# A two-layer block on one core: where powers, tables, quantised tiles and statistics stand among the projections

## The chip, the core and the metric

The kernel runs on one core of a Trainium2 chip. The metric is the device time of one execution in microseconds. The core has five engines that run side by side: TensorE (PE) multiplies matrices into PSUM, VectorE (DVE), ScalarE (ACT) and GpSimd (POOL) work on tiles in SBUF, and SyncE (SP) issues most transfers. Each engine runs its own list of instructions strictly in order.

## The reference, cut to what matters

The input `x` has 2 sequences of 4096 tokens with 512 channels. Layer 0 adds to `x` a gated state-space branch and a linear layer on quantised data; layer 1 adds a linear attention and a gated feed-forward part.

```python
xn = _layernorm(x, axis=-1)
# branch 1
x1 = xn @ w1_w.T + w1_b
x_conv = _silu(_depthwise_conv(x1, conv_w))        # three taps along the tokens
x_ssm = _ssm(x_conv, A, B_ssm, C_ssm, D_ssm)       # h = h*sigmoid(A) + x*B;  y = C.h + D*x
v = _silu(xn @ v1_w.T + v1_b)
branch1 = x_ssm * v @ w2_w.T + w2_b
# branch 2: rows of xn and of weight, rounded to 6-bit numbers by blocks of 32 with one scale each
branch2 = dequantised(xn) @ dequantised(weight).T + bias
x = x + branch1 + branch2
# layer 1 follows: layernorm, linear attention, gated feed-forward
```

## The kernel before, in words

All data is 32-bit. The tokens are cut into `NK` = 16 blocks of `T` = 512. The first stage, the projections, goes over the blocks `n`; after it come the recurrence (four groups of channels), and then for each sequence the mixing of both branches and layer 1. The change concerns the first stage alone, some 480 us of the 2400.

In block `n`, `projected` (L338) multiplies the normalised and transposed block `xnT` by `w1` and then by `v1`. Each product is four groups of 128 output channels; a group is gathered in one of four PSUM accumulators (`acc`) and copied out by ACT: `x1` (L351) for the first product, `v` with its Silu (L366) for the second. `tapped` (L394) makes the convolution of the block before: one ACT copy (L397), two DVE multiply-adds (L399), a Silu on ACT (L406), a DVE transpose (L408) and a store to `cd`. `halo` (L335) copies one column between neighbouring blocks on POOL.

Around the products, the other work of the stage:

- `fetched` (L290) loads the four token tiles of a block, three blocks ahead in the text. `measured` takes the mean and variance of two blocks (`layernorm_stats`, L123 and L124, and the chain of `rstd`, with a root on ACT, L110). `spread_out` (L132, L134) stores these numbers to DRAM and reads them back in another order into `mvi`.
- `laid` (L317) loads the same block a second time, in an order in which 32x32 transposes give the whole transpose. `turned` (L320) scales it on ACT by `mvi` (L128, sixteen pieces a block) and transposes it on DVE (L324, four a block) into the next `xnT`. Block 0 alone is transposed by TensorE.
- `chunk_powers` is a generator in three steps: powers of sigmoid(A) into `pw`; products of these in `cp` with sums and a store; then 64 small reads from DRAM into `a32` and `qc` (L252, L255). `chunk_tables` (L262, L266) transposes the results into tables `ta` and `tb` for the recurrence, one call for each of four groups of channels.
- `quantised_weight` quantises one of four tiles of branch 2's weight, and `quantised` one tile of 128 tokens; here the twelve tiles of blocks 0, 1 and 2. Both use `mx_scaled` (DVE L176 to L179, POOL L180) and `mx_rounded` (DVE L188 to L193, POOL L194).

Tiles of a pool with the same tag share a fixed number of places, handed out in the order of the text; a tile waits until the place it is to take is free. Tag `w` has four places of 8 KB a partition. Two hold `w1` and `v1` during the stage. The other two are taken in turn by `xi` of blocks 1 and 2 and then by `pw` and `cp`; `xi` of later blocks lies in two places of its own (tag `xi`). Tag `yv` has eight places, four of them taken by `xd0`, four left for tiles that are being quantised.

The order in each engine's list is not that of the text. A planner runs ahead of time over the whole program with its own estimates of durations: for each engine it takes, among the instructions that it believes ready, the one that stands earliest in the text. Later work thus fills free time, often some blocks ahead. Where a call stands in the loop therefore sets its rank and not its time, and the finished lists are kept even where the chip's times differ from the estimates.

The loop before:

```python
x1 = projected(work, n, xnT, x1)
if n % 2 == 0 and n + 2 < NK:
    measured(n + 2, xts.pop(n + 2) + xts.pop(n + 3))
    ...
if n + 1 < NK:
    xnT = turned(work, n + 1, xi)
if n in (2, 3, 8):
    next(powers)
elif 4 <= n < 4 + CC:
    chunk_tables(*made, n - 4)
    quantised_weight(work, n - 4)
if 6 <= n < 6 + 2 * TJ:
    ...                                   # one tile of blocks 0 and 1 each
if n in (NK - 3, NK - 2):
    ...                                   # two tiles of block 2 each
```

Of the kernel before, what the change touches and what calls it, by code (L numbers as in the profile page):

```python
# [10 lines left out]
F32 = mybir.dt.float32  # L11
# [6 lines left out]
P = 128  # L18
D = 512
CC = D // P  # L20
T = 512
TJ = T // P
# [21 lines left out]
def block_kernel(ctx: ExitStack, tc: tile.TileContext, a: dict, out: bass.AP):  # L44
# [5 lines left out]
    NK = B * NB  # L50
# [11 lines left out]
    single = ctx.enter_context(tc.tile_pool(name="single", bufs=1))  # L62
# [18 lines left out]
    def acc():  # L81
        return bank("acc", 4)
# [75 lines left out]
    def by_tile(wide):  # L158
        return wide[:, 0 : TJ * D].rearrange("p (j c t) -> p j c t", j=TJ, t=P)
# [100 lines left out]
    def chunk_tables(pw, kr, cc):  # L260

        nc.vector.transpose(  # L262
            window(ta[:, cc, 0, L - 1 : L], [[-1, L], [L, L]]),
            window(kr[:, cc, 0:1], [[1, L], [1, L]]),
        )
        nc.vector.transpose(  # L266
            tb[:, cc].rearrange("p c s -> p s c"),
            window(pw[:, cc * NS, L - 1 : L], [[L, NS], [-1, L]]),
        )
# [40 lines left out]

    def laid(work, n):

        if n < 3:
            xi = wp.tile([P, TJ, D], F32, tag="w", name="xi")
        else:
            xi = work.tile([P, TJ, D], F32, tag="xi", name="xi")
        nc.sync.dma_start(out=xi, in_=a["xi"][n * TJ : (n + 1) * TJ].rearrange("j p d -> p j d"))  # L317
        return xi

    def turned(work, n, xi):  # L320
        xnT = work.tile([P, CC, T], F32, tag="xnT", name="xnT")
        for j in range(TJ):
            laid_normalised(xi[:, j, :], mvi[:, :, n, j, :])
            nc.vector.transpose(  # L324
                xnT[:, :, j * P : (j + 1) * P], xi[:, j, :].rearrange("p (c t) -> p c t", t=P)
            )
        return xnT
# [11 lines left out]
    def projected(work, n, xnT, before):  # L339

        x1 = work.tile([P, CC, T + 2], F32, tag="x1", name="x1")
        tapping = []

        def finish():
            while tapping:
                tapping.pop(0)()

        for o in range(CC):
            pm = acc()
            product(pm, lambda k: w1[:, k, o * P : (o + 1) * P], lambda k: xnT[:, k, :])  # L350
            nc.scalar.activation(x1[:, o, 1 : T + 1], pm, AF.Identity, bias=w1_b[:, o, :])  # L351
            halo(n, o, x1, before)

            finish()
            if n:
                tapping.append(tapped(work, n - 1, before, o))
            if n == NK - 1 and o:

                tapping.append(tapped(work, n, x1, o - 1))
        if n == NK - 1:  # L360
            tapping.append(tapped(work, n, x1, CC - 1))
        for o in range(CC):
            pm = acc()
            product(pm, lambda k: v1[:, k, o * P : (o + 1) * P], lambda k: xnT[:, k, :])
            v = work.tile([P, T], F32, tag="v", name="v", bufs=3)
            nc.scalar.activation(v, pm, AF.Silu, bias=v1_b[:, o, :])  # L366
            nc.scalar.dma_start(out=vd[n, o], in_=v)
            finish()
        return x1

    def quantised_weight(work, o):
        y = yv.tile([P, D], F32, tag="yv", name="w_y")
        nc.sync.dma_start(out=y, in_=a["ffn_w"][o])
        s = mx_scaled(y)
        mx_rounded(y, s, work.tile([P, D], F32, tag="xe", name="w_c"))
        nc.vector.transpose(wd[:, :, o * P : (o + 1) * P], y)
# [625 lines left out]
    with tc.tile_pool(name="tab", bufs=1) as tab:  # L1002
        ta = tab.tile([P, CC, L, L], F32, name="ta")
        tb = tab.tile([P, CC, L, NS], F32, name="tb")
        qc = tab.tile([P, CC, L // 2, L], F32, name="qc")
        with pool("a", 2) as work, pool("pm", 1) as pm:
            xts = {0: fetched(work, 0)}
            w1 = load_weight("w1_w")
            ident = const.tile([P, P], F32, name="ident")
            make_identity(nc, ident)  # L1010
            w1_b = column("w1_b")
            v1 = load_weight("v1_w")
            v1_b, conv_w = column("v1_b"), column("conv_w", 3)
            xi = laid(work, 1)
            measured(0, xts[0])
            xnT = first_turned(work, xts.pop(0))
            xts[1] = fetched(work, 1)
            measured(1, xts.pop(1))
            spread_out(mvi[:, :, 1], sd[1], mv0[:, 1])
            xts[2] = fetched(work, 2)  # L1020
            spread_out(mvi[:, :, 0], sd[0], mv0[:, 0])
            d_ssm = column("D_ssm")
            abar, cb, b_ssm = (column(s, NS, pm) for s in ("A", "C_ssm", "B_ssm"))
            a32 = const.tile([P, CC, L // 2], F32, name="a32")
            ones = const.tile([P, 1], F32, name="ones")
            nc.gpsimd.memset(ones, 1.0)
            wd = const.tile([P, CC, D], F32, name="w_d")

            mask = const.tile([P, QC], F32, name="mask")
            nc.vector.tensor_reduce(  # L1030
                mask, ident.rearrange("p (q t) -> p q t", q=QC), AX.X, ALU.add
            )
            mask_c = const.tile([P, QC], F32, name="mask_c")
            nc.vector.tensor_reduce(
                mask_c, ident.rearrange("p (u q s) -> p q u s", u=2, q=QC), AX.XY, ALU.add
            )
            x1 = None
            made = []
            powers = chunk_powers(pm, made)
            xd0 = [yv.tile([P, CC, P], F32, tag="yv", name=f"xd{j}") for j in range(TJ)]  # L1040

            def quantise(m, j, dst):
                for _ in quantised(
                    m, j, dst, lambda: work.tile([P, D], F32, tag="xe", name="c")
                ):
                    pass

            for n in range(NK):
                if 0 < n < NK - 1:
                    xi = laid(work, n + 1)  # L1050
                if n + 3 < NK:
                    xts[n + 3] = fetched(work, n + 3)
                x1 = projected(work, n, xnT, x1)
                if n % 2 == 0 and n + 2 < NK:
                    measured(n + 2, xts.pop(n + 2) + xts.pop(n + 3))
                    for m in (n + 2, n + 3):
                        spread_out(mvi[:, :, m], sd[m], mv0[:, m])
                if n + 1 < NK:
                    xnT = turned(work, n + 1, xi)
                if n in (2, 3, 8):  # L1060
                    next(powers)
                elif 4 <= n < 4 + CC:
                    chunk_tables(*made, n - 4)
                    quantised_weight(work, n - 4)
                if 6 <= n < 6 + 2 * TJ:

                    m, j = divmod(n - 6, TJ)
                    if m == 1 and j == 0:
                        xd_b1 = by_tile(single.tile([P, CC * (T + 1)], F32, name="wide"))
                    quantise(m, j, lambda: xd_b1[:, j] if m else xd0[j])  # L1070
                if n in (NK - 3, NK - 2):

                    for j in range(2):
                        quantise(2, 2 * (n - NK + 3) + j, None)
                if n == NK - 2:
                    b_out = load_row("w2_b")
                    ffn_b = work.tile([P, D], F32, tag="xe", name="ffn_b")
                    nc.sync.dma_start(out=ffn_b, in_=a["ffn_b"].partition_broadcast(P))
                    nc.gpsimd.tensor_tensor(b_out, b_out, ffn_b, ALU.add)
                    bk, gamma, beta = (load_row(s) for s in ("bk", "gamma", "beta"))  # L1080
                    bq, mu_r, mu_k = column("bq"), column("mu_r"), column("mu_k")
                    om_r = const.tile([P, CC, 1], F32, name="om_r")
                    om_k = const.tile([P, CC, 1], F32, name="om_k")
                    nc.vector.tensor_scalar(om_r, mu_r, -1.0, 1.0, ALU.mult, ALU.add)
                    nc.vector.tensor_scalar(om_k, mu_k, -1.0, 1.0, ALU.mult, ALU.add)
        heads = [yv.tile([P, TL, L], F32, tag="yv", name=f"head{i}") for i in range(2)]
        with pool("s", 2) as work:
            recurrence(work, heads)
# [10 lines left out]
    for b in range(B):  # L1099
# [4 lines left out]
        made = (gt, ksum, load_weight("Wv"))  # L1104
        wq, wk1 = load_weight("Wq"), load_weight("W_k")
        c_wts = []
        if b + 1 < B:
            xd0 = [yv.tile([P, CC, P], F32, tag="yv", name=f"xd{j}") for j in range(TJ)]
# [90 lines left out]
```

## Time and profile before

| | |
|---|---|
| time, median of 3 runs | 2401.54 us (2398.27 to 2402.26) |
| profiled execution | 2401.88 us, span of the program 2400.1 us |
| busy share PE, DVE, ACT, POOL | 98%, 64%, 42%, 20% |
| projections on TensorE | 13.86 to 479.93 us |

Times inside the profile count from the start of the span. A row gives the start, the length, the engine, the line of the program, the operation, what it writes and reads, and how often it stands there in a row; in brackets is the time the engine was idle before it and who released it. TensorE takes each 32-bit product in two passes, so that the sixteen products of a half block show as `x32`.

### The profile page before, as it was taken

To read this page: it belongs to the slowest core of one execution; us is meant where nothing else is said; L and a number is where in the kernel's file an instruction comes from. 1 tells how busy PE (TensorE), PEld (TensorE's weight loads), DVE (VectorE), ACT (ScalarE), POOL (GpSimd) and SP (SyncE) were. 2 spreads that over 40 slices of the span, in tenths; PEclk is the share of its full clock that TensorE was granted. 3 is DMA by queue.
4 is the path that set the end of the run, shared out by engine and by line. 5 is a ranking of instruction groups with operands and counts; after the bars stand their busy time and mean duration, and the time that the engine had idled before them with its cause. 6 is when DMAs were issued, how large, how long until landed. Compare 5 with 4: busy or idle time off the path is not lost. (4 is left out here: it accounts for less than half of the span.)

```text
span 2400.1 us, 21969 instructions
## 1 busy us (share of the span) xinstructions
PE 2357.7 (98%) x6400; PEld 1105.2 (46%) x6400; DVE 1532.0 (64%) x3050; ACT 1018.5 (42%) x1933; POOL 477.8 (20%) x534
## 2 busy tenths in 40 slices
PE   7999999999999999999999999999999999999999
PEld 3334444466544444444444555444444444445554
DVE  6976864554486664257768778666652265557777
ACT  6766775334242333246763222133332236652222
POOL 0211220022143332110103112233332100001111
PEclk9999999999999999999999999999999999999999
DMA  7647432377843333202255435433432202264331
GB/s 262 197 130 229 137 141 96 115 223 251 317 132 113 110 117 94 67 28 104 92 210 194 149 134 189 165 108 115 119 110 75 62 31 88 90 217 141 126 133 57
DMA packets 253832, 328.12 MB, mean 137 GB/s; under 512 B 55952, under 2 KB 117392, under 8 KB 252688
## 3 DMA queue, kind: packets, MB, share of 16 engines
q1 hardware_dynamic: 224624, 259.59, 34.3%
q10 hardware_dynamic: 29088, 67.12, 7.2%
q8 instruction: 51, 0.84, 0.1%
q14 instruction: 69, 0.57, 0.1%
HBM read 205.38 MB, written 121.27 MB: 136 GB/s over the span
## 5 line engine op out<-in xcount | busy, mean ns | idle before, releaser
L154 PE MATMUL p_acc<-xnT,w_v_w 128*128 128x512 f32 x512 | 227.4, 600 | 9.1 <-ACT x L351 9.1
L154 PE MATMUL p_acc<-xnT,w_w_w 128*128 128x512 f32 x512 | 225.2, 597 | 9.4 <-DVE xnT L324 5.0
L698 PE MATMUL p_acc<-k,x 128*128 128x512 f32 x512 | 229.9, 592 | 0.9 <-ACT k L733 0.9
L154 PE MATMUL p_acc<-w_W_v,t 128*128 128x512 f32 x512 | 222.3, 592 | 0.0
L154 PE MATMUL p_acc<-w_W_r,xnT 128*128 128x512 f32 x448 | 201.4, 592 | 0.0
L154 PE MATMUL p_tr<-w_Wk,xnT 128*128 128x512 f32 x448 | 199.2, 592 | 0.2 <-ACT xnT L149 0.2
L971 POOL TENSOR_TENSOR x<-x,row_beta 128x512 f32<-128x512 f32 x64 | 84.1, 1314 | 552.5 <-ACT xn L128 542.2
L667 PE MATMUL p_mm<-w_w_w,t 128*128 128x512 f32 x416 | 186.7, 592 | 0.0
L110 ACT ACTIVATE rs_s<-rs_v 128x4 f32<-128x4 f32 (+1 forms) x41 | 8.4, 206 | 396.3 <-DVE rs_v L108 396.2
L652 PE MATMUL p_mm<-w_d,t 128*128 128x512 f32 x384 | 173.6, 593 | 1.2 <-DVE x L675 1.0
L154 PEld LDWEIGHTS p_acc<-xnT,w_v_w 128*128 128x128 f32 x512 | 97.9, 192 | 136.0 <-issue 116.5
L154 PEld LDWEIGHTS p_acc<-xnT,w_w_w 128*128 128x128 f32 x512 | 97.2, 191 | 135.2 <-issue 115.9
L696 POOL TENSOR_TENSOR ksum<-ksum,k 128x512 f32<-128x512 f32 x62 | 83.4, 1344 | 368.8 <-ACT k L733 368.8
L698 PEld LDWEIGHTS p_acc<-k,x 128*128 128x128 f32 x512 | 97.2, 190 | 123.7 <-issue 120.8
L154 PEld LDWEIGHTS p_acc<-w_W_v,t 128*128 128x128 f32 x512 | 97.3, 190 | 122.5 <-issue 118.9
L732 DVE TENSOR_TENSOR k<-p_tr,row_bk 128x512 f32<-128x512 f32 x64 | 43.8, 685 | 162.1 <-PE p_tr L154 162.1
L977 ACT ACTIVATE r<-p_acc 128x512 f32<-128x512 f32 x64 | 38.2, 597 | 246.1 <-PE p_acc L154 234.4
L399 DVE SCALAR_TENSOR_TENSOR xc<-x,col_conv_w,xc 128x512 f32<-128x512 f32 x128 | 99.5, 793 | 59.1 <-POOL x L335 33.9
L154 PEld LDWEIGHTS p_tr<-w_Wk,xnT 128*128 128x128 f32 x448 | 85.0, 190 | 107.6 <-issue 104.0
L180 POOL TENSOR_TENSOR xq<-xq,mx_rs 128x512 f32<-128x512 f32 x64 | 76.6, 1197 | 264.3 <-DVE mx_rs L179 197.8
L733 ACT ACTIVATE k<-k 128x512 f32<-128x512 f32 x64 | 40.1, 627 | 203.2 <-DVE k L732 184.6
L667 PEld LDWEIGHTS p_mm<-w_w_w,t 128*128 128x128 f32 x416 | 79.0, 190 | 99.5 <-issue 99.5
(223 smaller groups left out, 4057.5 us busy)
## 6 DMA issues: line engine op xcount, KB each, us to landing
x<-in_x SPq DMA_DIRECT2D x126, 256.0 KB, 3.5
vd<-v ACTq DMA_DIRECT2D x64, 256.0 KB, 2.6
cd<-xs SPq DMA_DIRECT2D x64, 256.0 KB, 2.0
xq<-in_xi SPq DMA_DIRECT2D x64, 256.0 KB, 4.4
xg<-cd SPq DMA_DIRECT2D x16, 1024.0 KB, 7.8
v<-vd SPq DMA_DIRECT2D x64, 256.0 KB, 4.6
xd<-x SPq DMA_DIRECT2D x64, 256.0 KB, 2.0
qd<-q ACTq DMA_DIRECT2D x64, 256.0 KB, 2.0
```

The lines of the kernel that those rows point to most:

```text
L110: nc.scalar.activation(s, v, AF.Sqrt)
L154: nc.tensor.matmul(out_ap, lhsT=lhsT(k), rhs=rhs(k), start=(k == 0), stop=(k == CC - 1))
L180: nc.gpsimd.tensor_tensor(by_block(y), by_block(y), rs.unsqueeze(2).to_broadcast([P, NQ, QB]), ALU.mult)
L399: nc.vector.scalar_tensor_tensor(xc, x1[:, cc, tap : tap + T], conv_w[:, cc, tap : tap + 1], xc, ALU.mult, ALU.add,)
L652: nc.tensor.matmul(po, lhsT=xds[i][j][:, k, :], rhs=wd[:, k, :], start=(k == 0), stop=False)
L667: nc.tensor.matmul(po, lhsT=z[:, k, j * P : (j + 1) * P], rhs=w2[:, k, :], start=False, stop=(k == CC - 1),)
L696: nc.gpsimd.tensor_tensor(ksum, ksum, kt, ALU.add)
L698: nc.tensor.matmul(pg[c], lhsT=xn[:, c * P : (c + 1) * P], rhs=kt, start=first, stop=last)
L732: nc.vector.tensor_tensor(kt, pk, bk, ALU.add)
L733: nc.scalar.activation(kt, kt, AF.Relu)
L971: nc.gpsimd.tensor_tensor(xt[j], xt[j], beta, ALU.add)
L977: nc.scalar.activation(r, pr, AF.Sigmoid)
```

## The change

`xi` of blocks 1 to 6, not only 1 and 2, lies in the places of tag `w`, so that `pw` and `cp` get theirs after these. In the loop, the call of `measured` with its stores and reads moves behind `turned`. The three steps of `chunk_powers` move from blocks 2, 3 and 8 to 6, 7 and 9, and the tables from blocks 4 to 7 to 8 to 11. The sixteen tiles to be quantised, so far in blocks 4 to 14 (the weight's in 4 to 7, those of blocks 0 and 1 in 6 to 13, of block 2 in 13 and 14), are set by a table: block 0's in blocks 1 to 4, block 2's first in 5, block 1's in 9 to 12, the weight's in 12 and 13, and the rest of block 2's in 13 and 14. No instruction is added or taken away.

```diff
     def laid(work, n):
-        if n < 3:
+        if n < 7:
             xi = wp.tile([P, TJ, D], F32, tag="w", name="xi")
...
+            beside = {
+                1: [(0, 0)], 2: [(0, 1)], 3: [(0, 2)], 4: [(0, 3)], 5: [(2, 0)],
+                9: [(1, 0)], 10: [(1, 1)], 11: [(1, 2)],
+                12: [("w", 0), ("w", 1), (1, 3)],
+                13: [("w", 2), ("w", 3), (2, 1)],
+                14: [(2, 2), (2, 3)],
+            }
+            xd_b1 = None
             for n in range(NK):
...
                 x1 = projected(work, n, xnT, x1)
+                if n + 1 < NK:
+                    xnT = turned(work, n + 1, xi)
                 if n % 2 == 0 and n + 2 < NK:
                     measured(n + 2, xts.pop(n + 2) + xts.pop(n + 3))
                     for m in (n + 2, n + 3):
                         spread_out(mvi[:, :, m], sd[m], mv0[:, m])
-                if n + 1 < NK:
-                    xnT = turned(work, n + 1, xi)
-                if n in (2, 3, 8):
+                if n in (6, 7, 9):
                     next(powers)
-                elif 4 <= n < 4 + CC:
-                    chunk_tables(*made, n - 4)
-                    quantised_weight(work, n - 4)
-                if 6 <= n < 6 + 2 * TJ:
...
-                    quantise(m, j, lambda: xd_b1[:, j] if m else xd0[j])
-                if n in (NK - 3, NK - 2):
...
-                        quantise(2, 2 * (n - NK + 3) + j, None)
+                if 8 <= n < 8 + CC:
+                    chunk_tables(*made, n - 8)
+                for what, j in beside.get(n, ()):
+                    if what == "w":
+                        quantised_weight(work, j)
+                    elif what == 0:
+                        quantise(0, j, lambda: xd0[j])
+                    elif what == 1:
...
+                        quantise(1, j, lambda: xd_b1[:, j])
+                    else:
+                        quantise(2, j, None)
```

More of the change, by code (lines that the diff above doesn't have):

```diff
@@ L1057, in block_kernel @@
                         spread_out(mvi[:, :, m], sd[m], mv0[:, m])
-                if n + 1 < NK:
-                    xnT = turned(work, n + 1, xi)
-                if n in (2, 3, 8):
+                if n in (6, 7, 9):
                     next(powers)
-                elif 4 <= n < 4 + CC:
-                    chunk_tables(*made, n - 4)
-                    quantised_weight(work, n - 4)
-                if 6 <= n < 6 + 2 * TJ:
-                    m, j = divmod(n - 6, TJ)
-                    if m == 1 and j == 0:
-                        xd_b1 = by_tile(single.tile([P, CC * (T + 1)], F32, name="wide"))
-                    quantise(m, j, lambda: xd_b1[:, j] if m else xd0[j])
-                if n in (NK - 3, NK - 2):
-                    for j in range(2):
-                        quantise(2, 2 * (n - NK + 3) + j, None)
+                if 8 <= n < 8 + CC:
[6 more added lines that the diff above has]
+                    elif what == 1:
+                        if xd_b1 is None:
+                            xd_b1 = by_tile(single.tile([P, CC * (T + 1)], F32, name="wide"))
+                        quantise(1, j, lambda: xd_b1[:, j])
+                    else:
+                        quantise(2, j, None)
                 if n == NK - 2:
```

## The prediction

> **What bounds the kernel now.** I read the page's busy table first, then TensorE's timeline over the projections, its waits there, the busy time by stretch, and last ACT, DVE and POOL around the gaps.
>
> ```profile
> PE 2357.7 (98%) x6400; PEld 1105.2 (46%) x6400; DVE 1532.0 (64%) x3050; ACT 1018.5 (42%) x1933; POOL 477.8 (20%) x534
> ```
>
> TensorE is the bound. Only time in which it idles, or runs slowly after idling, can be gained. TensorE's timeline (start, length, what, in brackets the idle time before it):
>
> ```profile
> 27.70 13.90 PE L154 MATMUL p_acc<-xnT,w_v_w 128*128 128x512 f32 x32
> 46.63 15.70 PE L154 MATMUL p_acc<-xnT,w_w_w 128*128 128x512 f32 x32 [5.04 <-DVE xnT L324]
> ...
> 78.01 14.00 PE L154 MATMUL p_acc<-xnT,w_w_w 128*128 128x512 f32 x32 [1.94 <-ACT v L366]
> ...
> 101.97 8.62 PE L154 MATMUL p_acc<-xnT,w_v_w 128*128 128x512 f32 x16 [3.10 <-ACT x L351]
> ...
> 199.23 13.90 PE L154 MATMUL p_acc<-xnT,w_w_w 128*128 128x512 f32 x32
> 212.96 13.90 PE L154 MATMUL p_acc<-xnT,w_v_w 128*128 128x512 f32 x32
> ...
> 302.05 12.51 PE L154 MATMUL p_acc<-xnT,w_v_w 128*128 128x512 f32 x24 [3.09 <-ACT x L351]
> ```
>
> An undisturbed half block takes 212.96 - 199.23 = 13.73 us. The 32 halves would take 439.5; they run from 13.86 to 479.93, which is 466.1. So 26.6 us are lost, and no version of this stage can gain more. By place, from the starts of the halves: blocks 0 to 1, 5.3 up to the start at 46.63 and 1.8 in the slow half after it; the rest of blocks 1 to 4 (46.63 to 171.66, eight halves) 13.4; blocks 5 to 8 only 0.1; block 9 to the end 6.0. Idle time alone is 17.7; what is left is matmuls that run longer after the gaps of 3 us and more.
>
> ```profile
> 43.00:78.00 35.00, 29.43 (x64) 12.67 (x64) 30.33 (x50) 23.19 (x49) 9.12 (x11) 0.95 0.58 186
> 78.00:108.00 30.00, 26.90 (x59) 11.83 (x60) 28.75 (x63) 23.40 (x50) 4.38 (x7) 0.94 0.76 263
> 108.00:136.00 28.00, 24.84 (x58) 10.39 (x57) 27.48 (x55) 16.87 (x32) 7.25 (x12) 1.00 0.47 130
> ...
> 164.00:192.00 28.00, 27.56 (x65) 12.06 (x65) 14.50 (x19) 19.94 (x41) 1.95 (x9) 1.00 0.52 135
> ...
> 220.00:247.00 27.00, 27.00 (x64) 11.93 (x64) 24.85 (x60) 16.20 (x31) 4.43 (x7) 1.00 0.76 251
> ...
> 358.00:385.00 27.00, 27.00 (x64) 11.97 (x63) 12.15 (x17) 15.87 (x32) 1.76 (x8) 1.00 0.32 117
> ```
>
> Columns: stretch, its length, busy PE, weight loads, DVE, ACT, POOL, granted clock, DMA. DVE needs 12.2 us a block for the taps and transposes alone; in the stretches that lose time it is 87 to 98% busy. But from 220 to 247 it is 92% busy, with statistics and quantised tiles, and TensorE loses nothing: it is the kind of filler that counts.
>
> **The first gap.** ACT, in its order:
>
> ```profile
> 29.30 2.02 ACT L128 ACTIVATE xi<-xi,mvi 128x128 f32<-128x128 f32 x5
> ...
> 33.34 1.28 ACT L110 ACT_TABLE_LOAD   x1
> ...
> 34.86 1.28 ACT L366 ACT_TABLE_LOAD   x1
> ...
> 38.78 0.48 ACT L128 ACTIVATE xi<-xi,mvi 128x128 f32<-128x128 f32 x1
> ...
> 44.19 8.57 ACT L128 ACTIVATE xi<-xi,mvi 128x128 f32<-128x128 f32 x22 [1.49 <-DMA xi<-in_xi]
> ```
>
> Block 1's sixteen L128 pieces start at 29.3, and twelve are done by 42.7. The root for the statistics of blocks 2 and 3, with two table loads, stands among them, and the last four come after 44.19, behind the store of the last `v`. TensorE was ready at 41.6.
>
> **The statistics behind the transposes.** Moved at each even block: eight times 0.66 + 0.17 on DVE and a chain of six small ones (7.6 us), one root with two table loads on ACT (1.28 + 0.21 + 1.28 = 2.77), ten DMAs on SP at about 0.43. In block 0 they now come after sixteen L128 and four transposes. ACT's remaining eleven pieces (0.41 each) and two `v` (0.69) then take 5.9 from 33.3: 39.2, ahead of 41.6 and of the store that held them. A transpose of 0.7 follows. The Trainium skill, "ScalarE: Activation LUTs", section "What ACT_TABLE_LOAD costs", counts 2.66 us for a switch, a drain included; here the root starts 1.30 after the load and `v` 1.30 after the next, with no drain to be seen. By the page 5.5 us leave ACT's way and the whole loss of 7.1 goes; by the row 2.8 leave, so a piece or two may still end behind the last `v`. I take the row: 1.5 of the 7.1 stays (ends 0 and 5), a gain of 5.6. What is late next: blocks 2 and 3 get their scales later. Before, from finished statistics (35.7) to the first use (44.2) was 8.5; from about 44 it is 52.5, and sixteen pieces between ACT's other work end near 63, against a need at 69. SP's sd store and mvi reads wait behind nothing longer than before. Costed at nothing, covered by those 6 us; beyond them each late us is one of TensorE's.
>
> **Powers, later.** Their two places are now taken in turn by blocks 1 to 6, so step one waits for block 5's turn (about 153 in this trace) and step two for block 6's (about 174). They leave block 1:
>
> ```profile
> 59.01 3.64 POOL L232 TENSOR_TENSOR cp<-pw,col_C_ssm 128x2048 f32<-128x2048 f32 x1 [5.43 <-issue]
> ```
>
> While this ran, a DVE instruction of 128x8 took 3.61 (others of its kind 0.17); the second such POOL product caught a tap for 3.51. With the sum of 3.72 and five products (2.9) they made ACT wait 4.99 and 4.45 for DVE, and TensorE 1.94 at 76. The four table pairs (L262 1.97, L266 1.04: 12 us) follow the powers; 2 us at a time ahead of the taps they stand before the 3.10 gap at 99 (DVE 92.46 to 96.7). SP's 64 small reads of `a_d` and `q_d` (0.48 each, 31 us, from 111 to 207) go behind block 6 too, and free SP for x and xi in blocks 3 to 6. In blocks 5 to 8, empty of loss today, all this finds a DVE of 14.5 to 18 in 28. I put 8 us there (ends 2 and 14: the whole 13.4 without the gap at the start is the most it cost before).
>
> **Quantised tiles.** Each costs DVE 3.9 us, POOL twice 1.05, ACT 1.65 (tiles of x), SP one load, the third block's also a store. Four of block 0 and one of block 2 go into blocks 1 to 5, the four of the weight to blocks 12 and 13. The planner fills free time, so more will be drawn forward than is written; four free `yv` places and SP's order bound it. Here a rule speaks against the change: the Trainium skill, "SBUF — State Buffer", section on the two separate sides, has GpSimd and a DVE instruction with two SBUF inputs exclude each other for the whole instruction. By it five tiles bring ten products, 10.5 us of closed port, into blocks 1 to 5, more than the 7.3 that the powers take out: no gain, 13 us stay. The row of 220 to 247 has such tiles and loses nothing, for a product of 1 us holds up one tap, and four accumulators cover it. I take 3 for blocks 1 to 4 (ends 0 and 13). The 6.0 of block 9 came from tiles in a row: SP waited up to 6.4 for a place, six tiles ended one after the other from 268 to 303, and a tap came 6.2 after ACT wanted it. Spread out they still queue: 2 (ends 0 and 6).
>
> **xi in other places.** Same loads; block 3's waits for block 1's turn instead of going at 36.8. SP stands until then, with x loads behind it that are needed much later: 0 (up to 2).
>
> **Sum.** 1.5 + 3 + 8 + 2 = 14.5 us of loss for 26.6: a gain of 12. The profiled execution took 2401.9 (span 2400.1 and 1.8 around it); the median is 2401.5, so the two agree. 2401.5 - 12 = 2389.5. The recurrence and all behind it keep their work, and the tables are ready well ahead of 480.
>
> **Rivals.** First: the gaps only move. The early blocks fill up with tiles as full as now, powers and tables stop TensorE in blocks 5 to 8 as they did in 1 to 4, and only the start is better: 20 to 21 us stay, 2396. For it: the planner's greed, seen in the statistics of blocks 10 and 11, done by 142, in block 3. Against: 220 to 275. Second, slower: in blocks 5 to 8 the tiles drawn forward, the powers with their closed port and the tables meet. Place: ACT's queue, where a Silu that waits for a late tap stands ahead of the copies that empty TensorE's accumulators. From a DVE demand over 27.5 us a block (12.2 + 3 tables + 7 powers + two tiles with their waits reach it) each block gives a gap of 3 to 5 plus 1.7 at slow clock; five such blocks lose 32, and with the start's gain still counted 33.5 in all: 7 more than now, 2408. For it: block 9's gap from tiles alone. Third: the start does not gain, since the store of `v` and not the root held the pieces: 5 us back on the first case, 2395.
>
> **Chances.** First case 0.45, gaps only moved or the start ungained 0.32, slower 0.23. A measurement of this kernel can tell about 0.2% (4.8 us) from no change. Faster by more: most of the first case and half of the second, 0.58; within: 0.20; slower: 0.22. Range 2378 (nearly all lost time back) to 2408.
>
> **What would show it.** Right: the gap at 41.6 under 2 us, no gap over 1 us up to block 4, `cp` products on POOL after 170, small gaps only behind them. Wrong: a gap of 3 us or more in blocks 5 to 9, or DVE still 95% busy from 46 to 136 with gaps; a wait of TensorE for `xnT` at block 2 would show the late scales.

## The result, and the profile after

The changed kernel takes 2396.94 us (median of 18 runs, 2393.78 to 2399.03), the one before 2402.07 in runs on the same chips. The ratio is 0.9978, 95% interval 0.9971 to 0.9985: faster by 5.1 us. The forecast was 12. The profiled execution after took 2395.06 us, 1.9 under its own median; its span is 2393.3 for 2400.1.

The busy table after:

```profile
PE 2356.1 (98%) x6400; PEld 1104.6 (46%) x6400; DVE 1530.0 (64%) x3050; ACT 1013.0 (42%) x1929; POOL 478.0 (20%) x534
```

TensorE's work is the same, and it still bounds. (ACT runs four instructions fewer: table loads of 1.28 us, 47 for 51.) TensorE's timeline over the projections, which now run from 14.01 to 472.74:

```profile
42.80 14.00 PE L154 MATMUL p_acc<-xnT,w_w_w 128*128 128x512 f32 x32 [1.06 <-DVE xnT L324]
...
120.29 7.42 PE L154 MATMUL p_acc<-xnT,w_v_w 128*128 128x512 f32 x16 [1.08 <-ACT x L351]
...
181.19 10.20 PE L154 MATMUL p_acc<-xnT,w_v_w 128*128 128x512 f32 x16 [3.37 <-ACT x L351]
191.22 13.90 PE L154 MATMUL p_acc<-xnT,w_w_w 128*128 128x512 f32 x32
...
210.39 3.70 PE L154 MATMUL p_acc<-xnT,w_v_w 128*128 128x512 f32 x8 [1.84 <-ACT x L351]
...
216.19 7.13 PE L154 MATMUL p_acc<-xnT,w_v_w 128*128 128x512 f32 x16 [2.10 <-ACT x L351]
...
328.09 7.13 PE L154 MATMUL p_acc<-xnT,w_v_w 128*128 128x512 f32 x16 [0.96 <-ACT x L351]
```

The gap at the start is 1.06 in place of 5.04, and most of the gaps of blocks 1 to 4 are gone. New ones stand at 181 (block 5) and at 210 to 216 (block 6). The same in stretches (length, busy PE, weight loads, DVE, ACT, POOL, granted clock, DMA):

```profile
42.80:156.30 113.50, 111.20 (x256) 48.22 (x257) 97.57 (x226) 90.57 (x190) 18.72 (x43) 1.00 0.77 246
164.00:192.00 28.00, 24.63 (x50) 10.47 (x51) 24.61 (x29) 19.25 (x38) 10.07 (x12) 0.88 0.35 85
192.00:220.00 28.00, 24.06 (x56) 10.29 (x55) 24.95 (x45) 12.68 (x25) 7.53 (x10) 1.00 0.39 123
```

The stretches after 164, where TensorE lost next to nothing before, are now those in which it loses. As a measure for every kernel I take TensorE's loss by block: from the start of a block's first product to that of the next, less 27.47 us (two undisturbed halves). One execution each:

| us lost in block | 0 | 1 to 4 | 5 | 6 | 7 to 11 | 12 to 15 | all |
|---|---|---|---|---|---|---|---|
| before | 5.3 | 15.2 | 0.1 | 0 | 6.0 | 0 | 26.6 |
| after | 1.3 | 3.7 | 7.5 | 4.7 | 2.1 | 0 | 19.3 |

The slow half at 46.63 before counts here under block 1. The loss fell by 7.3 and the span by 6.8, so the rest of the program hardly moved. Blocks 1 to 6 together lost 15.3 before and lose 15.9 now: the loss of the early blocks stands in blocks 5 and 6, and what the profile gained is 4.0 in block 0 and 3.9 in blocks 7 to 11.

### The profile page after: what moved, and what is told of

The parts are those of the page before. It is cut to its first block, busy times and chain, and to the rows that moved or that the text cites. A ratio compares the mean times of both kernels' runs of the same rounds, so it can differ in the third digit from the quotient of the medians.

```text
span 2393.3 us, 21964 instructions
## 1 busy us (share of the span) xinstructions
PE 2356.1 (98%) x6400; PEld 1104.6 (46%) x6400; DVE 1530.0 (64%) x3050; ACT 1013.0 (42%) x1929; POOL 478.0 (20%) x534
## 4 chain that ended last, share of the span: by engine, by line
PE 67%; DVE 4%; DMA 1%; ACT 1%; issue 1%; POOL 1%; SPq 0%; POOLq 0%; ACTq 0%; DVEq 0%
PE p_acc L154 18%; PE p_tr L154 9%; PE p_acc L698 8%; PE p_mm L667 7%; PE p_mm L652 7%; PE p_mm L823 6%; PE p_acc L823 6%; PE p_tr L823 2%; PE p_mm L950 1%; PE p_tr L950 1%; PE p_acc L652 1%; PE p_tr L652 1%; PE p_acc L667 1%; PE p_acc L488 0%; DVE t L886 0%
## 5 line engine op out<-in xcount | busy, mean ns | idle before, releaser
L399 DVE SCALAR_TENSOR_TENSOR xc<-x,col_conv_w,xc 128x512 f32<-128x512 f32 x128 | 95.7, 763 | 63.1 <-POOL x L335 30.9
```

Of the source, the lines that this page charges most:

```text
L399: nc.vector.scalar_tensor_tensor(xc, x1[:, cc, tap : tap + T], conv_w[:, cc, tap : tap + 1], xc, ALU.mult, ALU.add,)
```

## The experiments

Each ratio is against the kernel before, with its 95% interval; every kernel but the first is an edit of the changed one. Such losses by block are of one profiled execution, and they scatter, as the second run shows. A "tap" is one of DVE's multiply-adds of the convolution. Where an edit shifts the lines, L401, L404 or L406 is what is L399 in the changed kernel (the tap), and L408, L411 or L413 what is L406 there (the Silu).

### The statistics alone, and the same kernel again

In the kernel before, only the call of `measured` goes behind `turned`:

```diff
-                measured(n + 2, ...); spread_out(...)
                 if n + 1 < NK:
                     xnT = turned(work, n + 1, xi)
+                if n % 2 == 0 and n + 2 < NK:
+                    measured(n + 2, ...); spread_out(...)
```

> The kernel before with one part of the change alone: the statistics stand behind the transposes. If this order alone closed the first gap, TensorE's loss up to block 1 falls from 5.3 us to about 1.3, the slow half after it (1.8) goes, and the later gaps stay near 19.5 us in all: about 5.5 us faster than before, 0.9977. That would also mean that the moves of powers, tables and tiles brought next to nothing on balance. Rival: the start was freed by the later powers and the other layout places; then the gap at 41.6 stays at 4 to 5 us and the time is that of before.

Measured: 2402.14 us, 1.0 (0.9991 to 1.0008). TensorE's timeline of this kernel:

```profile
14.07 16.19 PE L154 MATMUL p_acc<-xnT,w_w_w 128*128 128x512 f32 x32 [0.67 <-ACT xnT L149]
...
44.47 14.00 PE L154 MATMUL p_acc<-xnT,w_w_w 128*128 128x512 f32 x32 [0.48 <-DVE xnT L324]
```

The gap at the start is 0.48, so this edit alone removes it. (The very first half ran slowly here, 16.19; eight of the eighteen profiled executions show that, the changed kernel in one of two.) But the total loss is 32.6: blocks 1 to 4 lose 16.9, blocks 7 to 11 12.6. This execution took 2407.53, 5.4 above the median of its kernel, so in a usual one some 27 would be lost (an estimate), as many as before. The start's gain was given back later; in which blocks a usual execution does so, and why, isn't shown.

The changed kernel a second time:

> The changed kernel unaltered, for a second profile of it and for its ratio on the same chip as the others. The first profile lost 19.3 us in the projections and lay 1.9 us under the median of its runs; if the slow clock after the 3.4 us gap (3.2 us) and the gaps depend on the execution, this one loses 19 to 22 with the same gaps at the same places. Ratio 0.9978.

Measured: 2397.18 us (16 runs), 0.9979 (0.9972 to 0.9987). Loss in block 0 4.1 (1.9 of it again a slow first half, 15.80; the gap at block 1's start 1.99), blocks 1 to 4 1.6, block 5 6.6, block 6 5.5, later 2.5; 20.3 in all. Blocks 5 and 6 together lose 12.2 and 12.1 in the two executions: that is no accident of one profile. Single blocks differ by up to 2.8 us.

### The powers back in the early blocks

```diff
-        if n < 7:
+        if n < 3:
...
-                if n in (6, 7, 9):
+                if n in (2, 3, 9):
```

> The kernel after with the powers back at blocks 2, 3 and 9 and the layout of only blocks 1 and 2 in the w places; tiles, tables and statistics stand as after. If moving the powers merely moved their loss, blocks 1 to 4 lose 8 to 12 us as before (13.4 there), blocks 5 and 6 about 1, and the time is that of after within 2 us (0.997 to 0.9985). If the later place was worth something by itself, it is slower than after by 4 us or more (0.9995 or above).

Measured: 2401.4 us, 0.9996 (0.9987 to 1.0004). Blocks 1 to 4 lose 12.1, block 5 4.1, block 6 nothing, later blocks 9.1; 26.5 in all. The powers bring their loss with them to where they stand: blocks 1 to 6 lose 16.2 in all, for 15.9 with the powers late. Without their move the changed kernel is as slow as the one before, and the difference in the profiles is block 9: it loses 8.5 here, where tiles stand in a row again (ACT waits 5.47 for a tap), and nothing in the changed kernel.

### The quantised tiles in their old order

```diff
-                1: [(0, 0)], 2: [(0, 1)], 3: [(0, 2)], 4: [(0, 3)], 5: [(2, 0)], ...
+                4: [("w", 0)], 5: [("w", 1)], 6: [("w", 2), (0, 0)], 7: [("w", 3), (0, 1)], ...
```

> The kernel after with the sixteen quantised tiles at the ranks they had before (the weight's in 4 to 7, the others in 6 to 14). If the new ranks matter, the early blocks are empty of tiles and lose under 1 us, but blocks 5 to 10 lose more: 16 us or more there, 4 us slower than after, 0.9995. If the planner's filling makes the ranks unimportant: the same within 2 us, 0.9978.

Measured: 2393.17 us, 0.9967 (0.9954 to 0.9979); block 5 10.1, block 6 nothing, 18.1 in all. The new order of the tiles brought nothing here; if anything it cost a little. The interval overlaps that of the changed kernel, and a later pair that differs by this order alone goes the other way (0.9953 with the new order, 0.9963 with the old), so the sign stays open.

### What happens in block 5: the products on POOL

DVE and ACT of the changed kernel around the gap at 181:

```profile
169.72 3.71 DVE L236 TENSOR_REDUCE kf<-cp 128x128 f32<-128x2048 f32 x1
...
174.00 3.62 DVE L237 TENSOR_TENSOR kf<-kf,col_D_ssm 128x4 f32<-128x4 f32 x1
...
178.80 0.74 DVE L399 SCALAR_TENSOR_TENSOR xc<-x,col_conv_w,xc 128x512 f32<-128x512 f32 x1
```

```profile
179.57 0.63 ACT L406 ACTIVATE xc<-xc 128x512 f32<-128x512 f32 x1 [4.82 <-DVE xc L399]
```

An addition on four columns takes 3.62 us: it starts just after the second product on POOL (L241, 173.51 to 177.59) and ends with it. The tap at 178.80 stands behind it, ACT waits 4.82 for that tap, and the copy that empties an accumulator stands behind the Silu. Three edits try this chain. The first puts POOL's two products in four pieces of 128x512 each:

```diff
-        nc.gpsimd.tensor_tensor(cp, pw, cbv, ALU.mult)
+        for c in range(CC):
+            g = slice(c * NS, (c + 1) * NS)
+            nc.gpsimd.tensor_tensor(cp[:, g], pw[:, g], cbv[:, g], ALU.mult)
...                                       # the second product alike
```

> The kernel after with the two POOL products of the powers (128x2048 each, 3.64 and 4.08 us) cut into four of 128x512. Theory of the closed port: each long product held a DVE instruction with two inputs for 3.6 us, which the planner does not count, and DVE's and ACT's lists ran late through blocks 5 and 6 (12.2 us lost). With pieces of about 1 us the taps get in between: 5 to 6 us lost there, some 6 us faster than after (ratio to before about 0.9953). Rival, the quantised tiles in a row (three from 195 to 208 ahead of a tap that ACT awaited for 10.2 us): blocks 5 and 6 lose the same within 2 us, ratio 0.9978.

Measured: 2400.58 us, 0.9989 (0.998 to 0.9997); block 5 7.3, block 6 9.4, so more in the two than in the changed kernel. Its POOL and its DVE:

```profile
176.10 3.75 POOL L246 TENSOR_TENSOR cp<-cp,col_A 128x512 f32<-128x512 f32 x3 [3.96 <-DVE kf L238]
179.80 0.18 POOL L340 COPY x<-x 128x1 f32<-128x1 f32 x1
```

```profile
176.59 1.02 DVE L239 TENSOR_TENSOR kf<-kf,col_D_ssm 128x4 f32<-128x4 f32 x1
...
180.01 1.51 DVE L404 SCALAR_TENSOR_TENSOR xc<-x,col_conv_w,xc 128x512 f32<-128x512 f32 x1 [1.48 <-POOL x L340]
```

The addition is held for 1.02 only. But the pieces stand back to back in POOL's list, the column copy of `halo` waits behind three of them, and the tap for the copy: DVE idles for 1.48 and then runs the tap in 1.51. The wait has moved from DVE's instruction to POOL's queue.

The second puts the products on DVE:

```diff
-        nc.gpsimd.tensor_tensor(cp, pw, cbv, ALU.mult)
+        nc.vector.tensor_tensor(cp, pw, cbv, ALU.mult)
...                                       # the second product alike
```

> The kernel after with the same two products on DVE instead of POOL: by the row of the largest powers product (128x1024 in 1.17 us) about 2.3 us each, in DVE's list where the planner counts them. Theory of the closed port: 4.6 us of counted work take the place of 7.2 us of uncounted waiting; blocks 5 and 6 lose 5 to 8 us in place of 12.2, about 5 us faster than after (0.9957). Rival (tiles in a row, or simply too much DVE work in two blocks): no gain, or a small loss, since DVE has more to do: 0.9978 to 0.9985.

Measured: 2393.8 us, 0.9965 (0.9952 to 0.9979); block 5 3.0, block 6 5.0, 16.3 in all. (Its interval overlaps that of the changed kernel.) DVE of this kernel:

```profile
174.28 0.11 DVE L237 TENSOR_TENSOR kf<-kf,col_D_ssm 128x4 f32<-128x4 f32 x1
174.31 2.28 DVE L241 TENSOR_TENSOR cp<-cp,col_A 128x2048 f32<-128x2048 f32 x1
```

The product takes 2.28 here and 4.08 on POOL, the addition 0.11 in place of 3.62. DVE has 4.6 us more to do, and block 5 loses less than half.

The third keeps the products on POOL and cuts DVE's sum (L236, 3.71) in four:

```diff
-        nc.vector.tensor_reduce(kf, cp.rearrange("p (c s) t -> p c t s", s=NS), AX.X, ALU.add)
+        for c in range(CC):
+            nc.vector.tensor_reduce(kf[:, c, :], cp[:, c * NS : (c + 1) * NS]..., AX.X, ALU.add)
```

> The kernel after with one edit: the long sum of the powers on DVE (128x2048 to 128x128, 3.7 us) in four of a quarter. If the length of a single DVE instruction ahead of a tap is what makes ACT wait in block 5, the gap of 3.4 us there shrinks to under 1.5 and blocks 5 and 6 lose 8 in place of 12: 3 to 4 us faster than after, 0.9963. If the amount of work counts and not its length: as after, 0.9978.

Measured: 2397.7 us, 0.9975 (0.9965 to 0.9984); block 5 6.1, block 6 6.7. The sum's length alone is not what holds the tap. Both together, products on DVE and products and sum in quarters:

> Products on DVE and, like the sum, in quarters; tiles and tables as after. Against the products on DVE in one piece (0.9965): if length counts, blocks 5 and 6 lose 3 to 4 in place of 8.0, ratio 0.995 or less, and the quarters are the main part of what the faster version had. If the old ranks of the tiles or the tables behind the taps were that part, it stays at 0.9965 (within 0.0007).

Measured: 2390.72 us, 0.9953 (0.994 to 0.9965); block 5 1.4, block 6 7.3, 14.2 in all. This is clearly faster than the changed kernel. Most of block 5's loss goes with the products, but the two blocks lose 8.7 together, not the 3 to 4 expected and no less than with the products in one piece (8.0): block 6's loss needs another cause.

### What happens in block 6: tiles drawn forward

ACT and DVE of the changed kernel ahead of the gaps at 210 and 216:

```profile
209.13 0.63 ACT L406 ACTIVATE xc<-xc 128x512 f32<-128x512 f32 x1 [10.16 <-DVE xc L399]
```

```profile
202.19 0.69 DVE L389 STREAM_TRANSPOSE wide<-xq 128x512 f32<-128x512 f32 x1
...
207.00 0.67 DVE L389 STREAM_TRANSPOSE wide<-xq 128x512 f32<-128x512 f32 x1
...
208.36 0.74 DVE L399 SCALAR_TENSOR_TENSOR xc<-x,col_conv_w,xc 128x512 f32<-128x512 f32 x1
```

Two tiles of block 1, written for blocks 9 to 12, run here in block 6, and a tile of the weight, written for block 12, has begun. They stand in DVE's list ahead of a tap that ACT awaits for 10.16 us: of the 10.9 us from 197.51 to the tap at 208.36, 2.48 are the transposes of `xnT`, 1.5 statistics, and nearly all the rest work on tiles. With the products on DVE ACT waits 12.02 there. Three edits try this. In the first the four tiles of block 1 are loaded, normalised and transposed, but not scaled and rounded:

```diff
-        scales = mx_scaled(xq)
+        plain = n == 1
+        scales = None if plain else mx_scaled(xq)
...
-        mx_rounded(xq, scales, temp())
+        if not plain:
+            mx_rounded(xq, scales, temp())
```

> The kernel after without the scaling and rounding of the four tiles of block 1 (they are only loaded, normalised and transposed): 3.2 us of DVE and two POOL products less for each. These are the tiles that stand from 177 to 208 in DVE's list ahead of the tap for which ACT waits 10 us. If they are the other part of the 12.2 us of blocks 5 and 6, block 6 loses under 2 in place of 4.7 to 5.5, 4 to 6 us faster than after in all: 0.9957. If the planner fills the room with the weight's tiles, or the tap is late anyway: 0.9975.

Measured: 2394.9 us, 0.9968 (0.9956 to 0.998). Block 6 loses 2.1, ACT's wait there is 5.05. But block 5 loses 10.5, so that both lose 12.5 as before, and the sum is 20.1. DVE of this kernel:

```profile
171.32 3.03 DVE L114 TENSOR_TENSOR rs_e<-rs_v,rs_r 128x8 f32<-128x8 f32 x1
...
179.15 3.60 DVE L237 TENSOR_TENSOR kf<-kf,col_D_ssm 128x4 f32<-128x4 f32 x1
```

In the new lists both products on POOL (170.69 and 178.65) catch a small instruction. The work came out of one block, and the planner's new lists put a worse collision into the other.

In the second, SP loads a tile only behind the last `cd` store of the block before the one where it is written:

```diff
                 for what, j in beside.get(n, ()):
+                  with behind(stored[n - 1, CC - 1]):
```

> The kernel after with one edit: the load of each quantised tile is queued on SP behind the last store of the block it is written in, so that the planner can't draw it forward. Theory of the tiles drawn forward: in blocks 5 and 6 four tiles stand in DVE's list ahead of the taps, on top of powers and tables, and ACT waits 10 us for a tap; without them blocks 5 and 6 lose 5 to 7 us in place of 12.2, blocks 3, 4 and 10 under 1 each: about 7 us faster than after, ratio 0.995. Rival, powers and tables alone make the loss: blocks 5 and 6 still lose 10 to 12, ratio 0.9975. Second rival: the tiles make new gaps in blocks 12 to 14, where three stand together: 1 to 3 us each there.

Measured: 2415.3 us, 1.0055 (1.0043 to 1.0068), clearly slower. Block 6 loses 2.9 and blocks 7 to 12 nothing, but block 5 loses 10.7 and blocks 13 to 15 16.5. The 5 to 7 expected of blocks 5 and 6 did not come: without the tiles they lose 13.6. ACT and TensorE of this kernel:

```profile
407.29 0.63 ACT L411 ACTIVATE xc<-xc 128x512 f32<-128x512 f32 x1 [7.04 <-DVE xc L404]
```

```profile
411.27 12.26 PE L154 MATMUL p_acc<-xnT,w_v_w 128*128 128x512 f32 x24 [2.68 <-ACT x L351]
```

From 394 to 408 two tiles of the weight and one of block 1 stand in DVE's list, nearly all of their work ahead of that tap. Three tiles in one block, as the table writes for blocks 12 and 13, cost more than they save when their loads also have to wait for the stores of the block before; the two are not told apart here. In the changed kernel the planner draws these tiles forward, and blocks 12 to 15 lose nothing.

In the third, the tables stand on DVE behind the last tap's transpose of the block before:

```diff
                 if 8 <= n < 8 + CC:
-                    chunk_tables(*made, n - 8)
+                    with behind(tapped_last[n - 1, CC - 1]):
+                        chunk_tables(*made, n - 8)
```

> The kernel after with one edit: each pair of tables is queued on DVE behind the last tap of the block it is written in (blocks 8 to 11); products on POOL and tiles as after. If the tables, 12 us of DVE drawn forward into blocks 4 to 6, are the other part of the 12.2 us lost in blocks 5 and 6, these lose 6 to 9 and the tables nothing in blocks 8 to 11: 3 to 5 us faster than after, ratio 0.9960. If the planner puts tiles into the room that the tables leave, blocks 5 and 6 keep 10 to 12: ratio 0.9978.

Measured: 2396.68 us, 0.9971 (0.996 to 0.9981); block 5 6.1, block 6 6.2, 21.4 in all. With all else as in the changed kernel, holding the tables back alone takes nothing from blocks 5 and 6.

### The cures together

Products on DVE with the tables held back as above:

> Both: the products on DVE and the tables queued behind the taps of their own blocks; tiles as after, free to be drawn forward. If closed port and tables add up, blocks 5 and 6 lose about 4 us as they did when the tiles were held back too, with no loss in blocks 12 to 15: stage loss 9 to 12, ratio 0.9945. If the tiles fill the room, 8 us stay there as with the products on DVE alone: 0.9965.

Measured: 2398.32 us, 0.9977 (0.9967 to 0.9986). Block 5 2.3, block 6 9.1, later 5.8: the two blocks lose 11.4, more than with the products on DVE alone (8.0). Products on DVE with the tiles in the old order:

> The products on DVE and the sixteen tiles at the ranks they had before the change; tables as after. If both gains add up (3.6 us from the products on DVE, 2.8 from the old ranks, each by its median against after), ratio 0.995. If both act on the same lateness of DVE in blocks 4 to 6, only the larger is had: 0.9965.

Measured: 2393.5 us, 0.996 (0.9947 to 0.9972); block 5 loses 3.5 and block 6 still 5.0. Products on DVE, tiles and tables both held back:

> The kernel after with the two products of the powers on DVE, the tiles gated as in the run before, and each pair of tables queued on DVE behind the last tap of the block it is written in. If closed port, tiles and tables together are the 12.2 us, blocks 5 and 6 lose 1 to 3 us, and the whole stage 5 to 8, most of it at the start: some 12 us faster than after, ratio 0.993. If the loss comes from elsewhere (the wait for places, the table loads on ACT), blocks 5 and 6 keep 5 us or more, ratio 0.996.

Measured: 2406.51 us, 1.0017 (1.001 to 1.0023), slower than before. Block 5 loses 4.0, blocks 6 to 11 nothing, and blocks 13 to 15 15.1: the price of the literal table again. That is 26.3 in all, as much as before; some 5 us more are lost just behind the stage, where TensorE waits 2.75 for a load of `cd`.

Products and sum on DVE in quarters, tables held back, tiles in the old order:

> A version meant to be faster: products on DVE in quarters of 128x512, the long sum (3.7 us) in quarters too, tables queued behind the taps of their blocks, tiles at the ranks from before. If what stops TensorE in blocks 4 to 6 is DVE work that is long in one piece or uncounted by the planner, these blocks lose 1 to 4 us and the stage 5 to 9: ratio 0.993. If the sheer amount of DVE work drawn forward does it, 8 to 10 us stay there: 0.9965.

Measured: **2389.97 us, 0.9945 (0.9933 to 0.9958)**, the lowest of all and faster than both kernels, though its interval overlaps that of the products and sum in quarters alone (0.9953): 12.5 us lost, 2.3 in block 5, none in block 6, 4.1 in block 10. Its stretches:

```profile
164.00:192.00 28.00, 26.29 (x61) 11.30 (x61) 27.70 (x54) 17.91 (x31) 4.41 (x10) 1.00 0.50 130
192.00:220.00 28.00, 28.00 (x66) 12.35 (x65) 16.25 (x23) 17.10 (x33) 3.13 (x14) 1.00 0.52 151
```

The columns are as above. From 164 to 192 DVE is busier than in the changed kernel (27.70 for 24.61), and TensorE gets 1.7 us more. The same without holding the tables back:

> The faster version (0.9945) with the tables free again: products and sum on DVE in quarters, tiles at the old ranks. If the gate on the tables did nothing, 0.9945 again within 0.0008; if the tables' 2 us pieces drawn forward still stop TensorE, blocks 4 to 6 lose 3 us or more above the 4.1 seen there, 0.996.

Measured: 2393.23 us, 0.9963 (0.995 to 0.9975); block 6 4.1, blocks 7 to 11 4.8, 20.1 in all. ACT of this kernel:

```profile
205.74 0.63 ACT L413 ACTIVATE xc<-xc 128x512 f32<-128x512 f32 x1 [8.37 <-DVE xc L406]
```

Between the tap at 194.05 and the one awaited, at 205.00, DVE's list has two table transposes (1.98 and 1.93), then a tile and the transposes of `xnT`. This pair of kernels differs by holding the tables back alone, and block 6 by 4.1; of the medians it makes 3.3 us, with intervals that just overlap. An edit's effect depends on the others, since each makes the planner write all lists anew.

Over all kernels with the powers late: with the products on POOL, blocks 5 and 6 together lose 10.1 to 16.7 us wherever tiles or tables stand. With the products on DVE they lose 6.3 to 11.4 as long as tiles or tables stand as in the changed kernel. Only the two kernels with the products on DVE, the tables held back and the tiles in other places too bring them down, to 4.0 and 2.3. Blocks 1 to 6 as a whole agree: 13.7 to 19.3, then 9.8 to 14.4, then 7.9 and 5.9. (With the old order of the tiles block 4 loses 4.4 to 4.9 as well, except in the best kernel.) Tiles and tables both held back with the products on POOL was not tried.

## Why the prediction was right or wrong

**The start: right.** 1.5 of 7.1 were to stay; the gap went from 5.04 to 1.06 (1.99 in the second execution), and no slow half came behind it. ACT of the changed kernel:

```profile
39.46 0.88 ACT L128 ACTIVATE xi<-xi,mvi 128x128 f32<-128x128 f32 x2
40.36 1.28 ACT L110 ACT_TABLE_LOAD   x1
41.65 0.21 ACT L110 ACTIVATE rs_s<-rs_v 128x8 f32<-128x8 f32 x1
41.88 1.28 ACT L366 ACT_TABLE_LOAD   x1
43.17 0.69 ACT L366 ACTIVATE v<-p_acc,col_v_b 128x512 f32<-128x512 f32 x1
```

All sixteen L128 pieces are now ahead of the root. Each load again takes 1.29 from its start to the next instruction, so the row was the one to take and not the 2.66, drain included, that the prediction quotes from the Trainium skill ("ScalarE: Activation LUTs", "What ACT_TABLE_LOAD costs"). The later scales cost nothing: TensorE did not wait for `xnT` at block 2. The third rival, an ungained start, falls.

**Blocks 1 to 4: right, taken alone.** 3 were to stay, measured 3.7 and 1.6. Tiles are drawn in, and DVE is busy for 97.57 of 113.50 us, but the row of 220 to 247 held. By the rule that GpSimd and DVE exclude each other, as the prediction quotes it, 13 would have stayed. The exclusion itself did show: in block 5 for 3.62 us beside a product of 4.08, and for a product of 1 us too (a DVE addition of 128x4 took 1.02 beside quarters of 128x512 on POOL). But holds of 1 us by the tiles cost TensorE little in blocks 1 to 4.

**Powers and tables in blocks 5 to 9: the step that failed.** The term was put at 8 us; measured were 12.2 and 12.1, within its ends of 2 and 14. With the 3 for blocks 1 to 4 the forecast was 11 in place of 15.3, and blocks 1 to 6 lost 15.9 (13.7 in the second execution): in these blocks the loss moved and did not shrink. The reasoning was that blocks with 14.5 to 18 us of DVE work in 28 have room. They have it on average. The kernel loses time by what stands ahead of one tap, and the room in the rest of the block doesn't help it. I had the row that mattered in hand (a DVE instruction of 128x8 that took 3.61 beside POOL's product) and took it as a part of a sum of work instead of as a block in the queue.

The parts of the 12, from the runs: the products on POOL make about 4 (both blocks lose 8.0 with them on DVE; block 5 alone 3.0 for 7.5 and 6.6). The rest is DVE work that the planner draws ahead of a tap in block 6. In the changed kernel that is tiles of block 1, which the prediction had charged to block 9 alone; with products and sum in quarters and the tiles in their old order it is tables and a tile. Taking out either tiles or tables alone left the two blocks at 12.3 to 13.6, so neither of them is a fixed part of the sum.

**Quantised tiles: size right by luck.** 2 were to stay in the queue of block 9; the changed kernel lost 1.9, in block 10. But with the old order that place lost no more (1.3 in blocks 7 to 11), and with the new order and the powers back early block 9 lost 8.5. So the gain there came with the later powers and not from the tiles' new order, to which the prediction put it.

**The sum.** 1.5 + 3 + 8 + 2 = 14.5 was forecast, 19.3 measured, and 4.2 of the 4.8 between them are the one step. The gain of 7.3 so left is 6.8 in the span and 5.1 in the medians, since the profiled execution lay 1.9 under its kernel's median: of the 6.9 us by which the gain of 12 was missed, some 2 are this scatter.

**The rivals.** The first was nearest, in its number (20 to 21 us, 2396) and in most of its reason: the gaps only moved, and powers, tables and tiles stop TensorE in blocks 5 and 6 as they did in 1 to 4. That the early blocks stay as full of gaps as before was wrong, and so was that only the start gets better (block 9 did too). The second has the mechanism that was seen, a Silu that waits for a late tap ahead of the copies, with a gap of 3.37 in block 5 and of 1.84 and 2.10 in block 6, but in two blocks and not in five. The sign named there (a gap of 3 us or more in blocks 5 to 9) came; the products on POOL ran at 163 and 174, the first somewhat ahead of the 170 named.

**Open.** Why the start's gain is lost again when only the statistics move; what is left in block 10 of the best kernel (4.1), why tiles in the old order leave block 6 empty in one kernel (0) and not in another (5.0, products on DVE); and how much of a difference of one or two us in a block is scatter.

## What to carry to other kernels

When work is moved to a stretch with room, do not compare sums of busy time: look for its longest instruction, and for each engine at what stands behind that instruction and whom the next engine serves. A POOL instruction of 4 us beside DVE's small ones was such a block here; giving it to DVE took away most of block 5's loss (3.0 left of 7.5, and 1.4 when cut up), while cutting it on POOL only moved the wait to POOL's queue. Where a planner fills free time, a place in the text is a rank: before trusting a new order, see from the trace where the work really runs, and after each edit look at the neighbouring blocks too: a loss that goes from one block often turned up in the next. Try edits in combination as well, since here their effects did not add.

## What was not expected of the hardware

A gap was dearer this time. Before, the matmuls behind the gaps of 3.10 and 5.04 us took 1.6 and 1.8 us longer than undisturbed ones, from their start to the next. Behind the gap of 3.37 after, sixteen passes took 10.03 (191.22 - 181.19) for 6.87 undisturbed (half of 13.73), with a granted clock of 0.88 between 164 and 192. So 3.2 of the 7.5 us lost in block 5 are matmuls that ran slowly behind one gap. Behind the gap of 2.10 only 0.3 was lost. The length of the gap alone does not decide: with the powers back early, a gap of 1.90 at 91.06 was followed by 1.8 us of such loss (clock 0.86 from 91 to 103.3), and in the run with products on DVE and tiles and tables held back, one of 2.42 (at 472.69) by 0.1.

The first half block took 14.00 us in ten of the eighteen profiled executions and 15.75 to 16.46 in the other eight, all with 0.67 or 0.68 us of idle time ahead of it.

DVE instructions of 128x8 or 128x4 took 3.61, 3.62, 3.60 and 3.03 us beside POOL products of 128x2048, and 0.11 to 0.20 in places where POOL ran no product beside them.
